# Local attention layers on one Trainium2 core: a list scheduler in place of a written order, the softmax maximum folded in by a matmul, one exponential per 128x512, the small norm steps on GpSimd

## The chip, the core and the metric

The kernel runs on one core of a Trainium2 chip. A core has five engines with queues of their own: TensorE (PE; PEld is its loading of weights), VectorE (DVE), ScalarE (ACT), GpSimd (POOL) and SyncE (SP), which here issues nearly all DMAs. Each engine takes its instructions in the order in which the program wrote them, and waits on semaphores for the others. The metric is the device time of one execution in microseconds (us); lower is better. Line numbers such as L804 are lines of the kernel before.

## What is computed

There are 32 batch elements of 128 rows and 128 features. First comes a cross attention with 16 heads of 8 features, with a layer norm in front, and then a stack of 6 layers. Each layer is a local attention with 16 heads of 64 features in windows of 32 rows, and a feed forward part. The core of the reference, cut:

```python
x = x + xattn(layernorm(x), ctx, ctx, ...)
y = layernorm(x)
for i in range(6):
    y = attn_layer(shift_tokens(y), Wqkv[i], ...) + y     # second half of the features from the row before
    y = ffn_layer(shift_tokens(y), ...) + y               # layer norm, a * gelu(gate), second product
out = x + y

# attn_layer: q, k, v = split(x @ Wqkv)
q = l2norm(q) * qs;  k = l2norm(k) * ksc                  # per head of 64
q = q * cos * scale + rotate_half(q) * sin * scale        # and k with 1 / scale
sim = einsum(q, k_window) * 8                             # own and previous window: 64 keys
attn = softmax(where(mask, -max, sim))
out = einsum(attn, v_window) @ Wo
```

## The kernel before, in words

**Tiles and stages.** All activations stay in one SBUF tile (`xt`). The batch is cut into 8 groups of 4 elements. The cross attention goes first, group by group; then the layers, each over the 8 groups. A **unit** is one batch element in one layer: 192 units, four to a group. While a layer runs, the weights of the next are loaded and prepared (`prep_ops`).

**A unit.** The group's input is transposed once: `ax` (L656) writes the first 64 features by PE transposes (L660) and the second 64 by a matmul with a shift matrix (L661), which also moves them down by one row. The result is split into a high and a low part, so that each large product is three 128x512 matmuls (`split3`, L634: L636, L637, L638). Four products give queries and keys (`qk`); each is squared on ACT (L686), summed per head on DVE (L689), multiplied with two tables on DVE (L694, two instructions) and added crosswise on POOL (L700). The sums of squares become a reciprocal square root (`rsqrt_a`, `rsqrt_b`, `rsqrt_c`): a maximum on DVE (L118), Ln and Exp on ACT (L126, L128), and one Newton step of three instructions on DVE (L133, L135, L137). POOL scales the four chunks (L723), PE transposes them (L729), and ACT and DVE copy them out (L735, L739, L744, L746).

**Values.** Value and output projection are one product (`yy`); ACT copies it out (L762) and 16 DMAs of 64 KB spread each window's rows over the partitions (L769).

**Softmax.** Half a unit is a block of 128x512 scores: a bf16 matmul writes the mask (L781), and 32 matmuls of 32 columns add the scores (L786). DVE takes the negated maximum of each 64 (L793). ACT runs eight exponentials of 128x64, each with its own bias column and its own accumulated sum (L804). DVE takes reciprocals (L809), POOL scales (L813), DVE transposes in 32x32 blocks (L817), and PE multiplies with the values in 28 matmuls (L830).

**Feed forward.** After four units the residual is added (L848), a DMA shifts the second half of the features by one row (L851, 127 partitions), the row norm follows (L857 to L880; its square root goes through the same helpers), then PE transposes, three gate products with Gelu on ACT (L910), three more products, and the second matrix (L935). After each Gelu group L912 loads the table set `natural_log_exp_and_others` again, which the kernel also loads at its start (L140).

**What sets the order.** The tables `OFF`, `GOFF`, `OFF1`, `GOFF1` (L38 to L84) give each operation of a unit a place on a time line, written out by hand. `push` puts functions with their times in a heap, and `drain` calls them in the order of time; each engine's queue follows from that. Buffers come from pools that rotate: five PSUM banks for products (`pj`), two for scores (`pscr`), one for the attention output (`pou`).

```python
        else:
            nc.scalar.activation(y, y, AF.Exp, scale=-0.5)
...
            for q in range(4 * half, 4 * half + 4):
                nc.scalar.activation(pr[:, q, :], scv[:, q, :], AF.Exp, bias=mx[:, q:q + 1],
                                     accum_out=ls[:, q:q + 1])
...
            if i == 2:
                nc.scalar.preload_act_table_set("natural_log_exp_and_others")
```

Of the kernel before, what the change touches and what calls it, by code (L numbers as in the profile page):

```python
# [8 lines left out]
F32 = mybir.dt.float32  # L9
# [7 lines left out]
P = 128  # L17
# [5 lines left out]
NRT = 8  # L23
NYT = 4
NKB = 3
NQT = 3
EWD = (1,)
STORE = 0.4
MP1 = [23.0 + 1.2 * i for i in range(8)]
WV1, DH1, DL1 = [20.85, 22.05], 0.15, 0.3  # L30
PREP0, PREPT = 10.0, 7.0
SHIFT = 6.0
FFT = 7.0
MP = [31.47, 31.72, 31.97, 32.22, 32.47, 32.72, 32.97, 33.22]
WV, BIAS, DH, DL = [24.4, 25.4], 16.4, 0.06, 0.14
T1 = 7.0
NI1 = 180
OFF1 = dict(  # L38
    sc=[[0, 2, 26, 28], [32, 34, 73, 75], [93, 95, 139, 141], [154, 159, 170, 172]],
    mx=[[1, 3, 27, 29], [33, 35, 74, 76], [94, 96, 140, 142], [158, 164, 171, 173]],  # L40
    sb=[[4, 5, 30, 31], [36, 37, 77, 78], [97, 98, 143, 144], [165, 168, 174, 175]],
    ex=[[39, 41, 44, 48], [99, 100, 101, 102], [151, 152, 155, 160], [187, 189, 192, 196]],
    tp=[[42, 46, 51, 55], [126, 127, 128, 129], [153, 157, 163, 167], [190, 194, 199, 203]],
    st=[[45, 50, 54, 57], [130, 132, 134, 135], [156, 162, 178, 179], [193, 198, 202, 205]],
    pa=[[49, 53, 82, 83], [131, 133, 136, 137], [161, 166, 186, 188], [197, 201, 218, 220]],
    oT=[[84], [138], [191], [223]], pb=[[145], [146], [195], [227]], rl=[[147], [148], [200], [232]],
    at=[[149], [150], [204], [236]],
)
GOFF1 = dict(
    ldc=[-101], gst=[-121, -120], gr0=[-119], gr1=[-117, -116], gr2=[-115, -114, -113], xa=[-118], xb=[-112],  # L50
    px=[-89], pxe=[-88], pcx=[-100], pce=[-99], pk=[-77], ke=[-76], kd=[-75], pq=[-74, -73, -71, -67],
    qe=[-72, -69, -65, -62], qd=[-70, -66, -63, -60], pv=[-55], vt=[-11], td=[-110], ab=[-109, -108], ln=[-4],
    mkb=[-56], tbm=[-3], p2=[238], aT=[249], pw=[265], rs=[266], hst=[267, 268], hr0=[269], hr1=[292, 296],
    hr2=[299, 301, 302], xf1=[270], xf2=[303],
)
T = 13.3
NI = 331
OFF = dict(
    qk=[[0, 1, 30, 31], [79, 80, 107, 108], [153, 154, 194, 195], [244, 245, 284, 285]],
    sq=[[2, 6, 32, 36], [81, 85, 109, 113], [155, 159, 196, 200], [246, 250, 286, 290]],  # L60
    ss=[[7, 11, 37, 41], [86, 90, 114, 118], [160, 164, 201, 205], [251, 255, 291, 295]],
    ta=[[3, 8, 33, 38], [82, 87, 110, 115], [156, 161, 197, 202], [247, 252, 287, 292]],
    tb=[[4, 9, 34, 39], [83, 88, 111, 116], [157, 162, 198, 203], [248, 253, 288, 293]],
    add=[[5, 10, 35, 40], [84, 89, 112, 117], [158, 163, 199, 204], [249, 254, 289, 294]],
    rs0=[[42], [119], [206], [296]], rs1=[[62, 63], [141, 142], [219, 220], [313, 314]],
    rs2=[[64, 65, 66], [143, 144, 145], [221, 222, 223], [315, 316, 317]],
    mul=[[67, 68, 69, 70], [146, 147, 148, 149], [224, 225, 226, 227], [318, 319, 320, 321]],
    tq=[[100, 102, 104, 136], [181, 183, 185, 228], [268, 270, 272, 275], [354, 356, 358, 381]],
    ev=[[101, 103, 105, 137], [182, 184, 186, 229], [269, 271, 273, 276], [355, 357, 359, 382]],
    ew=[[106, 138], [187, 230], [274, 277], [360, 383]],  # L70
    y=[[127, 128, 131, 150], [235, 236, 239, 281], [304, 305, 308, 328], [374, 375, 376, 407]],
    yt=[[129, 132, 134, 151], [237, 240, 242, 282], [306, 309, 311, 329], [384, 386, 388, 408]],
    dm=[[130, 133, 135, 152], [238, 241, 243, 283], [307, 310, 312, 330], [385, 387, 389, 409]],
    sc=[[124, 125, 178, 179], [216, 217, 260, 261], [301, 302, 347, 348], [390, 391, 426, 427]],
    mx=[[126, 180], [218, 262], [303, 349], [392, 428]],
    ex=[[165, 166, 212, 213], [256, 257, 297, 298], [343, 344, 377, 378], [422, 423, 451, 452]],
    rl=[[167, 214], [258, 299], [345, 379], [424, 453]], pl=[[168, 215], [259, 300], [346, 380], [425, 454]],
    PT=[[231, 232], [322, 323], [402, 403], [470, 471]], av=[[263, 264], [350, 351], [429, 430], [506, 507]],
)
GOFF = dict(  # L80
    ax=[-53], axh=[-52], axl=[-51], res=[508], psh=[564], fst=[565, 596], xn1p=[598], frs0=[597], frs1=[655, 656],
    frs2=[657, 658, 683], xn2p=[684], ptn=[735], xnh=[736], xnl=[737], gate=[831, 832, 833], gel=[834, 835, 836],
    pa=[850, 851, 853], um=[852, 854, 855], w2=[869, 870, 871, 872], res2=[873],
)  # L84

@with_exitstack
def body(ctx: ExitStack, tc: tile.TileContext, x, ctx_in, fside, mask, xWq, xWk, xWv, xWo, xtw,
# [5 lines left out]
    NG = B // GB  # L93
    HC = [(0, 128), (128, 128), (256, HID - 256)]
    RT = HC[2][1]

    const = ctx.enter_context(tc.tile_pool(name="const", bufs=1))
    small = ctx.enter_context(tc.tile_pool(name="small", bufs=4))

    nC = cst.shape[1] - 512  # L100
    cs = const.tile([P, nC], F32, tag="cs", name="cs")
# [5 lines left out]
    shift = cs[:, 516:644]  # L107
    identb = const.tile([P, P], BF16, tag="identb", name="identb")
    nc.vector.tensor_copy(identb, ident)
    maskb = const.tile([P, 512], BF16, tag="maskb", name="maskb")  # L110
    xt = const.tile([P, B, P], F32, tag="xt", name="xt")

    def rsqrt_a(src, n, eps, floor, tagp):
        v = small.tile([P, n], F32, tag=tagp + "v", name=tagp + "v")
        if eps is not None:
            nc.vector.tensor_scalar(v, src, eps, None, op0=ALU.add)
        else:
            nc.vector.tensor_scalar(v, src, floor, None, op0=ALU.max)  # L118
        y = small.tile([P, n], F32, tag=tagp + "y", name=tagp + "y")
        t = small.tile([P, n], F32, tag=tagp + "t", name=tagp + "t")  # L120
        return v, y, t

    def rsqrt_b(a, c):
        v, y, t = a
        if c == 0:
            nc.scalar.activation(y, v, AF.Ln)  # L126
        else:
            nc.scalar.activation(y, y, AF.Exp, scale=-0.5)  # L128

    def rsqrt_c(a, c):  # L130
        v, y, t = a
        if c == 0:
            nc.vector.tensor_tensor(t, y, y, op=ALU.mult)  # L133
        elif c == 1:
            nc.vector.scalar_tensor_tensor(t, v, -0.5, t, op0=ALU.mult, op1=ALU.mult)  # L135
        else:
            nc.vector.scalar_tensor_tensor(y, t, 1.5, y, op0=ALU.add, op1=ALU.mult)  # L137
        return y

    nc.scalar.preload_act_table_set("natural_log_exp_and_others")  # L140

    wch = ctx.enter_context(tc.tile_pool(name="wch", bufs=1))
    wst = ctx.enter_context(tc.tile_pool(name="wst", bufs=1))
    pj = ctx.enter_context(tc.tile_pool(name="pj", bufs=5, space=PSUM))
    pscr = ctx.enter_context(tc.tile_pool(name="pscr", bufs=2, space=PSUM))
    pou = ctx.enter_context(tc.tile_pool(name="pou", bufs=1, space=PSUM))

    heap = []
    seq = [0]

    def push(t, fn, a):
        heapq.heappush(heap, (t, seq[0], fn, a))
        seq[0] += 1

    def drain():
        while heap:
            _, _, fn, a = heapq.heappop(heap)
            fn(*a)

    NU = NG * GB  # L160
    ws = [None] * (L + 1)

    def prep_ops(l):
        w = ws[l] = {"qk": [None] * 4, "m": [None] * 4}
        wqk = Wqkv[l]
        V = {}

        def ld(i):
            if i == 0:
                V["w1r"] = wst.tile([P, 2 * HID], F32, tag="stg", name="w1r", bufs=2)  # L170
                nc.sync.dma_start(V["w1r"], W1[l])
            elif i == 1:
                V["col"] = wst.tile([P, 2], F32, tag="lgb", name="lgb")
                nc.sync.dma_start(V["col"][:, 0:1], ln_g[l].unsqueeze(1))
            elif i == 2:
                nc.sync.dma_start(V["col"][:, 1:2], ln_b[l].unsqueeze(1))
            elif i == 3:
                w["b1"] = wch.tile([P, 2, 3], F32, tag="b1c", name="b1c", bufs=2)
                nc.vector.memset(w["b1"], 0.0)
                for s in range(2):  # L180
                    nc.sync.dma_start(w["b1"][:, s, 0:2],
                                      b1[l, s * HID:s * HID + 2 * P].rearrange("(i p) -> p i", p=P))
            elif i == 4:
                nc.sync.dma_start(w["b1"][0:RT, :, 2], b1[l].rearrange("(s h) -> h s", s=2)[2 * P:HID])
            elif i == 5:
                w["w2"] = wch.tile([P, 3, P], F32, tag="w2", name="w2", bufs=2)
# [849 lines left out]
```

## Time and profile before

| | |
|---|---|
| median of 3 runs | 3326.27 us (3325.03 to 3327.11) |
| span of the profiled execution, first to last instruction | 3320.9 us |
| mean granted TensorE clock | 0.994 |
| ACT: exponentials (L804) and their accumulator reads | 3072 x 331 ns and 3072 x 225 ns |
| ACT: table loads at L910, L912 and L140 | 48 + 48 + 1, 1283 ns each |
| DVE: table products (L694) | 1536 x 681 ns |
| DVE: first step of the norm chain (L118) | 192 x 857 ns |
| PE: shift matmuls (L661) and their transposes (L660) | 384 x 298 ns and 192 x 293 ns |
| POOL: crosswise sum (L700), scaling (L723), softmax scaling (L813) | 768 x 1286, 768 x 1043, 384 x 1044 ns |
| DMA of the value rows (L769) | 3072 of 64 KB |

How to read it: the span is 5.4 us shorter than the median of the runs, which also counts what lies around the program. Durations are means over one profiled execution. The spans of PE overlap, since its matmuls are pipelined, and their ends are modelled: for PE the distance between starts tells more than the duration. An idle gap is put down to the semaphore that came last.

### The profile page before, as it was taken

How to read it: one execution, taken by the hardware profiler on the slowest of the kernel's cores; microseconds unless marked ns; L12 is line 12 of the kernel's file. 1: busy time of each engine (PE TensorE's matmuls, PEld its weight loads, DVE VectorE, ACT ScalarE, POOL GpSimd, SP SyncE). 2: the span in 40 equal slices, each digit the busy share in tenths (PEclk: the TensorE clock that was granted, in tenths of full speed). 3: DMA queues.
4: the chain of work that ended last, by engine and by line, in shares of the span. 5: the costliest groups of instructions: out<-in, count | busy, mean ns of one | idle time of the engine just before them, and what ended most of it. 6: DMA issues, size and time to landing. Idle time of an engine off the chain costs nothing.

```text
span 3320.9 us, 102077 instructions
## 1 busy us (share of the span) xinstructions
PE 3155.8 (95%) x35979; PEld 2389.3 (72%) x35979; DVE 2979.5 (90%) x6954; ACT 2834.9 (85%) x9983; POOL 2468.3 (74%) x2284
## 2 busy tenths in 40 slices
PE   8999899999999999999999999999999999999997
PEld 5555677777777777777777777777777777777775
DVE  6666899999999999999999998998999998999995
ACT  6776888898888898889898889898888898898895
POOL 5655777777787777787787787786787776777873
PEclk9999999999999999999999999999999999999998
DMA  2110333332333332233332333332333332333332
GB/s 61 33 37 12 77 87 82 79 74 71 75 83 86 78 74 72 72 85 84 77 77 71 75 83 81 79 77 68 79 83 76 84 76 64 77 82 81 82 83 62
DMA packets 217966, 243.80 MB, mean 73 GB/s; under 512 B 83534, under 2 KB 112498, under 8 KB 217458
## 3 DMA queue, kind: packets, MB, share of 16 engines
q1 hardware_dynamic: 217026, 236.93, 28.8%
q8 instruction: 288, 4.72, 0.6%
q14 instruction: 220, 1.80, 0.2%
q10 hardware_dynamic: 432, 0.34, 0.0%
HBM read 25.31 MB, written 4.19 MB: 9 GB/s over the span
## 4 chain that ended last, share of the span: by engine, by line
PE 49%; DVE 32%; ACT 8%; issue 4%; DMA 3%; SPq 2%; POOL 1%; ACTq 0%; DVEq 0%; POOLq 0%
DVE t L694 10%; PE pO L830 8%; PE ptq L729 7%; DVE ss L689 6%; PE sc L786 4%; DVE rnv L118 3%; PE pa L542 3%; PE pqk L636 3%; PE pqk L638 3%; ACT pr L804 3%; PE pqk L637 3%; DVE mx L793 2%; DVE PT L817 2%; SPq L769 2%; PE py L636 2%
## 5 line engine op out<-in xcount | busy, mean ns | idle before, releaser
L700 POOL TENSOR_TENSOR rt<-t,t 128x512 f32<-128x512 f32 x768 | 980.3, 1286 | 372.8 <-DVE t L694 330.8
L694 DVE TENSOR_TENSOR t<-pqk,tab 128x512 f32<-128x512 f32 x1536 | 983.3, 681 | 115.9 <-ACT sq L686 110.3
L804 ACT ACTIVATE pr<-sc,mx 128x64 f32<-128x64 f32 x3072 | 915.7, 331 | 61.2 <-DVE PT L817 53.0
L723 POOL TENSOR_TENSOR rt<-rt,rny 128x512 f32<-128x512 f32 x768 | 777.4, 1043 | 214.1 <-DVE rny L137 213.4
L804 ACT ACTIVATION_READ_ACCUMULATOR pr<-sc,mx 128x1 f32 x3072 | 691.9, 225 | 0.0
L689 DVE TENSOR_REDUCE ss<-sq 128x8 f32<-128x512 f32 x768 | 517.4, 674 | 0.0
L830 PE MATMUL pO<-ysh,PT 128*32 128x128 f32 x10752 | 416.9, 275 | 53.3 <-DVE PT L817 48.7
L813 POOL TENSOR_TENSOR pr<-pr,rl 128x512 f32<-128x512 f32 x384 | 400.8, 1044 | 89.2 <-DVE rl L809 89.2
L686 ACT ACTIVATE sq<-pqk 128x512 f32<-128x512 f32 x768 | 429.3, 600 | 24.6 <-PE pqk L638 12.5
L830 PEld LDWEIGHTS pO<-ysh,PT 128*32 128x32 f32 x10752 | 367.1, 110 | 97.6 <-DVE PT L817 72.1
L762 ACT COPY yt<-py 128x512 f32<-128x512 f32 x768 | 416.8, 614 | 21.2 <-PE py L638 17.2
L729 PE MATMUL ptq<-cs,rt 128*128 128x128 f32 x3072 | 409.8, 278 | 22.2 <-DVE t L694 17.0
L729 PEld LDWEIGHTS ptq<-cs,rt 128*128 128x128 f32 x3072 | 334.5, 141 | 96.7 <-issue 52.5
L786 PE MATMUL sc<-kb,qT 128*32 128x128 f32 (+1 forms) x12288 | 375.1, 262 | 15.2 <-DVE kb L744 14.8
L786 PEld LDWEIGHTS sc<-kb,qT 128*32 128x32 f32 x12288 | 270.7, 109 | 114.5 <-issue 70.7
L636 PE MATMUL py<-mw,xsh 128*128 128x512 f32 x768 | 333.1, 434 | 8.9 <-ACT yt L762 5.8
L636 PE MATMUL pqk<-wqh,xsh 128*128 128x512 f32 x768 | 314.0, 409 | 4.8 <-ACT yt L762 2.8
L638 PE MATMUL py<-mw,xsl 128*128 128x512 f32 x768 | 301.9, 393 | 0.0
L638 PE MATMUL pqk<-wqh,xsl 128*128 128x512 f32 x768 | 300.9, 392 | 0.0
L637 PE MATMUL pqk<-wql,xsh 128*128 128x512 f32 x768 | 300.8, 392 | 0.0
L637 PE MATMUL py<-mw,xsh 128*128 128x512 f32 x768 | 300.6, 391 | 0.0
L735 ACT COPY qT<-ptq 128x512 f32<-128x512 f32 x384 | 208.1, 590 | 79.0 <-PE ptq L729 78.1
(168 smaller groups left out, 5756.8 us busy)
## 6 DMA issues: line engine op xcount, KB each, us to landing
ysh<-yt SPq DMA_DIRECT2D x3072, 64.0 KB
raw<-in_L_ffn_Wqkv SPq DMA_DIRECT2D x36, 256.0 KB
xsu<-xt SPq DMA_DIRECT2D x48, 127.0 KB
wor<-in_L_ffn_Wo SPq DMA_DIRECT2D x6, 512.0 KB
xt<-in_x SPq DMA_DIRECT2D x8, 256.0 KB
cx<-in_ctx SPq DMA_DIRECT2D x8, 256.0 KB
mk<-in_mask_BxS_ff SPq DMA_DIRECT2D x8, 256.0 KB
x_scratch<-xt SPq DMA_DIRECT2D x8, 256.0 KB
```

What stands on the lines that cost most here:

```text
L636: nc.tensor.matmul(pt, lh, rh, start=True, stop=False)
L637: nc.tensor.matmul(pt, lh, rl, start=False, stop=False)
L638: nc.tensor.matmul(pt, ll, rh, start=False, stop=True)
L686: nc.scalar.activation(V["sq", c], V["pp", c], AF.Square)
L689: nc.vector.tensor_reduce(V["ss"][:, c * 8:(c + 1) * 8], V["sq", c].rearrange("p (h d) -> p h d", d=64), axis=AX.X, op=ALU.add)
L694: nc.vector.tensor_tensor(V["t", k, c].rearrange("p h s d -> p h (s d)"), V["pp", c].rearrange("p (h d) -> p h d", d=64), w["tab"][:, c // ...
L700: nc.gpsimd.tensor_tensor(V["rt", c], V["t", 0, c], V["t", 1, c][:, :, ::-1, :], op=ALU.add)
L723: nc.gpsimd.tensor_tensor(rv, rv, V["rn"][:, c * 8:(c + 1) * 8].unsqueeze(2).to_broadcast([P, 8, 64]), op=ALU.mult)
L729: nc.tensor.transpose(V["ptq", c][:, k, :], V["rt", c][:, 2 * k:2 * k + 2].rearrange("p h s d -> p (h s d)"), ident)
L786: nc.tensor.matmul(sc[32 * c:32 * c + 32, :, wd, lo:64], qT[:, c, 32 * wd:32 * wd + 32], kT[:, c, :, 32 * wd - 32 + lo:32 * wd + 32], star ...
L804: nc.scalar.activation(pr[:, q, :], scv[:, q, :], AF.Exp, bias=mx[:, q:q + 1], accum_out=ls[:, q:q + 1])
L830: nc.tensor.matmul(pO[32 * wd:32 * wd + 32, j, :], PT[:, half, wd, blk, :], ysh[u][:, (2 * par + half) * P:(2 * par + half + 1) * P], star ...
```

## The change

Nearly every line of `body` is rewritten; what is computed stays. What is different:

- `Sched` takes every operation with its engine, what it reads and writes, a priority (the unit's number, shifted by the table `LATER`) and a cost from the table `COST`. It plays the program through once and at each moment starts the most urgent operation that is ready and for which a buffer is free. That order is the program's order, and the buffers handed out are the program's buffers. It counts 1.3 us for a change between the Gelu table (`G`) and the table of the exponentials and logarithms (`E`).
- PSUM: six banks for products, one for scores, one for the attention output.
- Scores: the negated maximum is written as float32r, and a matmul of the identity with the maximum, broadcast over 64 columns, adds it to the scores (`fold`). One exponential of 128x512 follows. DVE then sums each 64 (`sm`), in place of the accumulated sums.
- Norm chain: `newton` runs the maximum (or the added epsilon) and the Newton step, now four instructions, on POOL; Ln and Exp stay on ACT.
- The two table products become one DVE instruction of 128x1024 (`tab`).
- The second half of the keys is always copied by ACT.
- The shifted half lives in columns 128 to 192 of `xt`. The group input is transposed by four PE transposes. The shift by one row is now always a pair of DMAs, of 112 and of 15 partitions, once before the feed forward and once for the next layer.
- The table set `natural_log_exp_and_others` is loaded by name once, at the start; the line after the Gelus is not there.

```diff
-            nc.vector.tensor_scalar(v, src, floor, None, op0=ALU.max)
-            nc.scalar.activation(y, v, AF.Ln)
-            nc.scalar.activation(y, y, AF.Exp, scale=-0.5)
-            nc.vector.tensor_tensor(t, y, y, op=ALU.mult)
-            nc.vector.scalar_tensor_tensor(t, v, -0.5, t, op0=ALU.mult, op1=ALU.mult)
-            nc.vector.scalar_tensor_tensor(y, t, 1.5, y, op0=ALU.add, op1=ALU.mult)
+                nc.gpsimd.tensor_scalar(sl(v), cols(), floor, None, op0=ALU.max)
+            nc.scalar.activation(sl(y), sl(v), AF.Ln)
+            nc.scalar.activation(sl(y), sl(y), AF.Exp, scale=-0.5)
+            nc.gpsimd.tensor_tensor(sl(t), sl(y), sl(y), op=ALU.mult)
+            nc.gpsimd.tensor_tensor(sl(t), sl(t), sl(v), op=ALU.mult)
+            nc.gpsimd.tensor_scalar(sl(t), sl(t), -0.5, 1.5, op0=ALU.mult, op1=ALU.add)
+            nc.gpsimd.tensor_tensor(sl(y), sl(y), sl(t), op=ALU.mult)
...
-                nc.tensor.transpose(G["ptx"][0:64, k, :], xb[:, 0:64], ident)
-                nc.tensor.matmul(G["ptx"][64:128, k, :], xb[:, 64:128], shift, start=True, stop=True)
+        S.op("ax", lambda: tr4(pt.t, [xsg(g)[:, k] for k in range(GB)]), pri, [X[g], XS[g]], [pt], also=[hi, lo])
...
-            nc.vector.tensor_tensor(V["t", k, c].rearrange("p h s d -> p h (s d)"),
-                                    V["pp", c].rearrange("p (h d) -> p h d", d=64),
-                                    w["tab"][:, c // 2, k, :].unsqueeze(1).to_broadcast([P, 8, 64]), op=ALU.mult)
+            S.op("tab", lambda: nc.vector.tensor_tensor(
+                t.t.rearrange("p (k h d) -> p k h d", k=2, d=64),
+                pp.t.rearrange("p (h d) -> p h d", d=64).unsqueeze(1).to_broadcast([P, 2, 8, 64]),
+                tab.t[:, c // 2].unsqueeze(2).to_broadcast([P, 2, 8, 64]), op=ALU.mult), pri, [pp, tab], [t])
...
-            for q in range(4 * half, 4 * half + 4):
-                nc.scalar.activation(pr[:, q, :], scv[:, q, :], AF.Exp, bias=mx[:, q:q + 1],
-                                     accum_out=ls[:, q:q + 1])
+                S.op("fold", lambda: nc.tensor.matmul(sc.t, identr, mx.t.unsqueeze(2).to_broadcast([P, 8, 64]), start=False,
+                                                      stop=True, skip_group_check=True), pri, [mx, sc], [sc])
+                S.op("ex", lambda: nc.scalar.activation(pr.t, sc.t, AF.Exp), pri, [sc], [pr], table="E")
+                S.op("sm", lambda: nc.vector.tensor_reduce(sm.t, r8(pr), axis=AX.X, op=ALU.add), pri, [pr], [sm])
...
-            nc.sync.dma_start(xsu[1:P], xg[0:P - 1, :, 64:128])
+            nc.sync.dma_start(xt[g][1:113, :, 128:192], xt[g][0:112, :, 0:64])
+            nc.sync.dma_start(xt[g][113:P, :, 128:192], xt[g][112:P - 1, :, 0:64])
...
-            if i == 2:
-                nc.scalar.preload_act_table_set("natural_log_exp_and_others")
```

The core of the scheduler's step, with the charge for a table:

```python
                occ = o.occ
                if o.table and o.table != table:
                    table = o.table
                    occ += 1.3
                    if table == "G":
                        hold = 3
...
                end = t + o.done + occ - o.occ
                free[e] = t + occ
                heapq.heappush(times, free[e])
                order.append((t, o))
```

## The prediction

> **What bounds the kernel now.** I read the busy shares first, then the steady stretch, then the order of matmuls inside it, because busy shares of four engines between 74% and 95% do not say which one sets the pace.
>
> ```profile
> PE 3155.8 (95%) x35979; PEld 2389.3 (72%) x35979; DVE 2979.5 (90%) x6954; ACT 2834.9 (85%) x9983; POOL 2468.3 (74%) x2284
> ```
>
> The profiled execution spans 3320.9 us; the median of the runs is 3326.27, so 5.4 us lie around the span. From 700 to 2700 us only the layer stage runs. In that window the groups give:
>
> ```profile
> 700.00:2700.00 2000.00, 1928.65 (x23101) 1494.78 (x23100) 1869.55 (x3775) 1769.69 (x6447) 1540.77 (x1416) 1.00 0.32 77
> ```
> ```profile
> L813 POOL TENSOR_TENSOR pr<-pr,rl 128x512 f32<-128x512 f32 x259 | 270.4, 1044 | 59.3 <-DVE rl L809 59.3
> L118 DVE TENSOR_SCALAR rnv<-ss 128x32 f32<-128x32 f32 x130 | 111.1, 855 | 4.5
> ```
>
> The columns of the first are the length, then busy time of PE, PEld, DVE, ACT, POOL. L813 runs twice per unit (one batch element in one layer), so 129.5 units pass in 2000 us: **15.44 us per unit**. Per unit DVE is busy 14.4 us, ACT 13.7, POOL 11.9. PE shows 14.9, but its spans overlap, so I take starts instead:
>
> ```profile
> 1498.28 0.40 PE L638 MATMUL pqk<-wqh,xsl 128*128 128x512 f32 x1
> 1498.52 0.39 PE L781 MATMUL sc<-maskb,identb 128*128 128x512 bf16 x1
> 1498.84 0.97 PE L786 MATMUL sc<-kb,qT 128*32 128x64 f32 x32
> 1499.74 0.50 PE L636 MATMUL py<-mw,xsh 128*128 128x512 f32 x1
> 1500.08 0.39 PE L637 MATMUL py<-mw,xsh 128*128 128x512 f32 x1
> 1500.31 0.40 PE L638 MATMUL py<-mw,xsl 128*128 128x512 f32 x1
> ```
>
> Full matmuls start 0.23 us apart. Behind the 32-column score matmuls the first pair is 0.34 apart instead (1499.74 to 1500.08). Over this window the gap from the last small matmul to the next full one is 0.20, against 0.03 within a small run; and a full matmul before unmasked small ones holds PE 0.32. So a change from small to full costs 0.17 + 0.11 = **0.28 us**, full to small 0.09. I priced the whole queue of the window with the median gap of each neighbour pair (clean means within small runs): 14.2 us per unit. PE has 14.2 us to issue and takes 15.44: it is the bound, with 1.24 us of waits on engines nearly as full (DVE 14.4, ACT 13.7).
>
> **The change, part by part** (per unit; 192 units, four to a group).
>
> *PE, work.* The shift matmuls of the group input go: before, four pairs of transpose and two-pass matmul take 4 x (0.23 + 0.16 + 0.20) = 2.37 us a group; four transposes at 0.11 take 0.44. That is -0.48 per unit. The fold of the maximum adds two 128x512 matmuls at 0.23: +0.46. Nothing in the trace shows one with a broadcast moving operand: below 0.23 there is no reason to go, the 0.43 spacing of the L435 matmuls would be the top (+0.4 more); it has the shape and type of L636, so 0.23.
>
> *PE, order.* The list scheduler interleaves more finely. In the instruction order, runs of one kind rise from 10.0 to 16.2 per unit; the two attention products stand apart (28 small matmuls each, before 56 together), and the halves of a score block are split. Small to full rises from 0.8 (0.5 after scores, 0.3 after the shift and weight pieces) to 3.85: 3.0 x 0.28 = +0.85. Full to small without a mask rises from 0.4 to 3.0: +0.23. Small to transpose (0.23 each) falls from 1.5 to 1.0, small to mask rises by 0.3, the rest nets to nothing: -0.05. Sum about +1.03; pricing the changed order instruction by instruction gives 15.25 against 14.2, **+1.05** with the two work terms. 1.3 us of the 15.25 rests on pairs not seen before, priced by their nearest.
>
> *ACT.* Eight exponentials with their accumulator reads take 0.29 each, 4.64 for 16; two 128x512 ones at the 0.49 of the squares take 0.98: -3.66. The key copy that leaves DVE adds 0.58. Then the table loads. The line that restored the combined table after each Gelu (L912) is gone, and the built order now has 231 loads before the Ln of the norm chains, 248 before exponentials and 48 before Gelu: 528 against 97, from 0.5 to about 2.8 per unit. What one costs:
>
> ```profile
> 1508.25 0.24 ACT L804 ACTIVATION_READ_ACCUMULATOR pr<-sc,mx 128x1 f32 x1
> 1508.51 1.28 ACT L910 ACT_TABLE_LOAD   x1
> 1509.81 1.83 ACT L910 ACTIVATE u<-pg,b1c 128x512 f32<-128x512 f32 x3
> 1511.65 1.28 ACT L912 ACT_TABLE_LOAD   x1
> 1512.95 1.07 ACT L735 COPY qT<-ptq 128x512 f32<-128x512 f32 x2
> ```
>
> From the end of one operation to the start of the next are 1.32 us (1508.49 to 1509.81), and neighbours that otherwise overlap by 0.11 no longer do: 1.43. So 2.25 x 1.43 = +3.2, and ACT stays at 13.7 - 3.66 + 0.58 + 3.2 = **13.8**: the relief is spent. The Trainium skill ("ScalarE: Activation LUTs", What ACT_TABLE_LOAD costs) puts a switch of sets at about 2.66 us, load and drain; that would add 6.0, make ACT 16.6 and the bound at 17.5 or more a unit. The row decides for 1.43. The same page (Table sets) has one set with both exp and ln, and the trace agrees: before, Ln and Exp follow each other 0.26 us apart with no load.
>
> *DVE and POOL.* DVE loses the norm chain (0.855 + 0.490 + 0.243 + 0.192 = 1.78, and some 0.56 for the group's), a key copy 0.69, and 0.25 from one double-width product per chunk; the sums of the exponentials add 1.25. About 12.4. POOL gets five steps of 128x32 and, per group, five of 128x4. No row has them: MEMSETs of 1 to 16 columns take 0.10 to 0.12; the line through 128x256 (0.616) and 128x512 (1.043) gives 0.24 and 0.20, which I take; as slow as DVE's they would be 1.8. +1.45, to 13.4. The skill speaks against it ("GPSIMD Engine Reference", Performance versus the Vector engine: elementwise about twice as slow there). Double the fastest DVE passes (0.235, 0.146, 0.191, 0.191) is 1.53, about the same sum. But the median rnv takes 0.85 against a fastest 0.235, so the DVE steps mostly stood and waited; "SBUF — State Buffer" (Who interferes with whom) names a port that DVE and GpSimd lock for each other, which fits.
>
> That chain now holds POOL's queue: the Ln and the Exp stand behind loads, so 1.4 to 2.9 us more pass between its first and second step, while the median order leaves POOL 2.2 us of other work there. Behind the waiting step stand the scalings of four rotated chunks, on which PE's transposes wait. Cover: PE has 20 us of its own work between a unit's projections and its first transpose. I charge this nothing alone; without that cover it is up to 1.5 a unit.
>
> *SP.* The shift of rows becomes two DMAs, of 112 and 15 rows, and is made for the next layer too: 192 issues for 48. At 0.6 to 0.76 us each +90 us on a queue whose 3072 value copies take 1,800 of 3320: hidden; behind a shift that waits for its residual stand value copies of the next unit, two units of buffers ahead. The copy of 127 rows takes 10.4 us from issue to use at the end (3288.37 to 3298.74); the value copies in the chain of waits take 2.6 to 2.9. I take 3, so the exposed tail falls 8 us; 0 if it stays. The cross attention keeps its work and has no added loads: 0, within 8 us either way. One score bank instead of two, and six projection banks instead of five, are inside the waits below.
>
> **The sum.** PE's issue is 15.25. For the waits I keep the measured 1.24: ACT is as full as before (13.8), POOL fuller (13.4), DVE emptier, and the loads are in no cost of the scheduler's table. 16.5 per unit, 192 x 1.05 = +202; 3320.9 + 5.4 + 202 - 8 = **3520 us**.
>
> **The rivals.**
> - *Loads hidden* (0.2). The order leaves a median 4.3 us of PE work between a projection or transpose and the reuse of its bank, and ACT needs about 0.9 of it. Then waits fall to some 0.4: 15.65, +40, and 3360 with the tail. Against it: the score bank has only 2.3 us between fold and reuse.
> - *Loads stop PE* (0.18). Ln and Exp with both loads hold ACT 3.2 us while every bank waits. If each pair, 1.2 per unit, adds 1 us on top of the old waits, 17.7: 3750.
> - *Faster* (0.12). One mechanism: at the 3.85 places where full matmuls follow small ones, the gap is a disguised wait and not a price. It decides when the 0.28 is under 0.08 and waits are at 0.4: then 14.5 + 0.5 = 15.0, 3235. Against it: the 0.20 and 0.34 are nearly constant over the window. At 15.4 it breaks even.
> - *Nothing moves* (0.03): small gaps and waits cancel, about 3326.
> - The forecast has 0.47, with waits from 0.8 to 1.9: 3435 to 3645.
>
> A measurement of this kernel can tell about 0.2% from no change. Faster 0.12, same 0.03, slower 0.85. The range cuts off the faster case and the upper end of the loads case: 3340 to 3740.
>
> **What would show it.** Right: about 528 table loads of 1.28 us, ACT busy near 80 to 90%, POOL idle before its second norm step on ACT, PE gaps of 0.20 and 0.34 behind small matmuls some 3.9 times a unit, a fold at 0.23 spacing, units of 16.5 us. Wrong: units under 15.4, PE's priced queue well under 15.25, no loads before Ln and Exp, or ACT under 70%.

## The result, and the profile after

| | before | changed |
|---|---|---|
| median | 3325.65 us (4 runs, 3324.52 to 3327.11) | 3717.3 us (4 runs, 3709.44 to 3729.36) |
| ratio | 1 | 1.1181, 95% interval 1.116 to 1.1203 |
| profiled execution, its span | 3320.9 us | 3729.36 us, span 3727.6 us |
| mean granted TensorE clock | 0.994 | 0.975 |

The change costs 392 us. The forecast was 3520, 194 us more than before: the sign was right, the size was half. Line numbers from here on are those of the changed kernel, except where the kernel before is named. First the busy shares of the changed kernel's page, then its answer for 700 to 2700 us (length; busy PE, PEld, DVE, ACT, POOL; granted clock):

```profile
PE 3395.6 (91%) x35979; PEld 2387.0 (64%) x35979; DVE 2613.5 (70%) x5157; ACT 2821.4 (76%) x4846; POOL 2736.2 (73%) x3528
```
```profile
700.00:2700.00 2000.00, 1834.27 (x20235) 1305.82 (x20234) 1431.14 (x2291) 1563.99 (x2642) 1510.00 (x1940) 0.98 0.30 71
```

Every engine is busy for a smaller share of the time than before: all of them wait for each other. POOL's softmax scaling (L817, twice a unit) runs 227 times in the window, so 113.5 units pass: 17.62 us a unit for 15.44. Per unit ACT is busy 1563.99 / 113.5 = 13.8, POOL 13.3, DVE 12.6. The table loads are there, in the costliest groups of the page:

```profile
L376 ACT ACT_TABLE_LOAD x231 | 296.4, 1283 | 4.1
L379 ACT ACT_TABLE_LOAD x225 | 288.7, 1283 | 4.0
...
L872 ACT ACT_TABLE_LOAD x48 | 61.6, 1283 | 0.9
L814 ACT ACT_TABLE_LOAD x23 | 29.5, 1283 | 6.1 <-PE bank__67 L812 3.9
```

L376 is the Ln of the norm chain, L379 its Exp, L872 Gelu, L814 the softmax exponential. How they reach PE is seen in selected rows of one passage of the timeline (start, duration, engine, line, instruction; in brackets the idle time before it and what ended it):

```profile
1429.76 1.28 ACT L376 ACT_TABLE_LOAD   x1
1429.80 0.29 POOL L373 TENSOR_SCALAR rv__18192<-ss__17849 128x32 f32<-128x32 f32 x1
...
1430.52 0.19 DVE L816 RECIPROCAL sm__18174<-sm__18174 128x8 f32<-128x8 f32 x1
...
1431.06 0.23 ACT L376 ACTIVATE ry__18194<-rv__18192 128x32 f32<-128x32 f32 x1
1431.31 1.28 ACT L379 ACT_TABLE_LOAD   x1
1432.60 0.23 ACT L379 ACTIVATE ry__18194<-ry__18194 128x32 f32<-128x32 f32 x1
...
1432.91 0.24 POOL L382 TENSOR_TENSOR rw__18207<-ry__18194 128x32 f32<-128x32 f32 x1 [2.83 <-ACT ry__18194 L379]
1433.11 1.26 POOL L748 TENSOR_TENSOR rt__18149<-t__18190 128x512 f32<-128x512 f32 x1
1434.33 1.04 POOL L817 TENSOR_TENSOR pr__18095<-pr__18095,sm__18174 128x512 f32<-128x512 f32 x1
1434.40 0.60 ACT L814 ACTIVATE pr__18178<-bank__67 128x512 f32<-128x512 f32 x1
1435.40 0.71 DVE L819 STREAM_TRANSPOSE PT__18243<-pr__18095 128x512 f32<-128x512 f32 x1 [1.82 <-POOL pr__18095 L817]
1436.17 0.30 PE L829 MATMUL bank__68<-ysh__17703,PT__18243 128*32 128x128 f32 x1 [3.07 <-DVE PT__18243 L819]
```

ACT spends 1429.76 to 1432.83 on two loads and two operations of 0.23 us. POOL has done the first norm step (L373) and stands 2.83 us before the second (L382). Behind it in POOL's queue is the softmax scaling L817 of another block. Its last operand was ready at 1430.71 (the reciprocal L816), and it starts at 1434.33; so the transpose L819 is late, and PE stands 3.07 us before the products with the values. And PE pays once more. The same answer by windows, for that stretch and the two after it:

```profile
1429.50:1436.20 6.70, 3.21 (x31) 2.03 (x22) 4.88 (x8) 6.38 (x11) 3.79 (x7) 1.00 0.03 7
1436.50:1439.90 3.40, 3.40 (x43) 2.08 (x36) 3.40 (x6) 0.00 (x0) 3.15 (x6) 0.50 0.00 0
1439.90:1450.00 10.10, 10.10 (x144) 7.07 (x143) 7.63 (x13) 8.36 (x16) 9.00 (x9) 1.00 0.29 67
```

After the stall the granted clock is 0.50 for 3.4 us (third column from the right). The trace has 39 stretches at 0.50, of 3.4 us or longer, for 7 before; (1 - 0.975) x 3727.6 = 93 us of clock are lost for 20.

**Where the 407 us between the two spans are.** The first mask matmul of the layers comes at 363.6 us for 332.6 (+31: the cross attention). From there to the last mask matmul pass 3327.4 us for 2941.4 (+386, 2.0 a unit). The rest to the end takes 36.6 for 46.9 (-10).

### The profile page after: what moved, and what is told of

Read it like the earlier page. It is cut to its first block, busy times and chain, and to the rows that moved or that the text cites. A ratio compares the mean times of both kernels' runs of the same rounds, so it can differ in the third digit from the quotient of the medians.

```text
span 3727.6 us, 95891 instructions
## 1 busy us (share of the span) xinstructions
PE 3395.6 (91%) x35979; PEld 2387.0 (64%) x35979; DVE 2613.5 (70%) x5157; ACT 2821.4 (76%) x4846; POOL 2736.2 (73%) x3528
## 3 DMA queue, kind: packets, MB, share of 16 engines
q14 instruction: 175, 1.43, 0.1%
## 4 chain that ended last, share of the span: by engine, by line
PE 43%; ACT 18%; DVE 15%; POOL 11%; issue 10%; DMA 3%; SPq 1%; ACTq 0%; POOLq 0%; DVEq 0%
PE bank__68 L829 5%; PE bank__67 L803 4%; ACT L376 3%; ACT L379 2%; PE bank__67 L687 2%; PE bank__67 L812 2%; PE bank__62 L403 1%; PE bank__63 L403 1%; PE bank__65 L409 1%; PE bank__61 L403 1%; SPq L784 1%; PE bank__61 L409 1%; PE bank__64 L403 1%; PE bank__67 L799 1%; PE bank__65 L403 1%
## 5 line engine op out<-in xcount | busy, mean ns | idle before, releaser
L799 PE MATMUL bank__67<-maskb,identb 128*128 128x512 bf16 x384 | 150.4, 392 | 36.7 <-ACT pr__25002 L814 3.1
L799 PEld LDWEIGHTS <-identb 128*128 128x128 bf16 x384 | 37.2, 97 | 77.4 <-issue 76.9
L839 DVE TENSOR_TENSOR xt<-bank__68,xt 128x512 f32<-128x512 f32 x48 | 32.6, 679 | 2.8 <-PE bank__68 L829 2.6
L770 ACT COPY kb__85<-bank__63 64x512 f32<-64x512 f32 x36 | 20.8, 578 | 11.0 <-PE bank__63 L409 11.0
L770 ACT COPY kb__85<-bank__65 64x512 f32<-64x512 f32 x31 | 17.8, 574 | 12.0 <-PE bank__65 L409 11.9
L770 ACT COPY kb__85<-bank__62 64x512 f32<-64x512 f32 x39 | 22.5, 577 | 3.5 <-PE bank__62 L409 3.4
L770 ACT COPY kb__85<-bank__64 64x512 f32<-64x512 f32 x32 | 18.4, 575 | 7.4 <-PE bank__64 L409 7.4
L770 ACT COPY kb__85<-bank__61 64x512 f32<-64x512 f32 x29 | 16.7, 578 | 8.7 <-PE bank__61 L409 8.6
L895 DVE TENSOR_TENSOR xt<-bank__61,xt 128x512 f32<-128x512 f32 x10 | 6.9, 692 | 23.2 <-PE bank__61 L891 23.2
L771 ACT COPY kb__85<-bank__62 64x512 f32<-64x512 f32 x39 | 22.7, 581 | 0.6
L895 DVE TENSOR_TENSOR xt<-bank__62,xt 128x512 f32<-128x512 f32 x9 | 6.2, 691 | 23.1 <-PE bank__62 L891 23.1
L895 DVE TENSOR_TENSOR xt<-bank__66,xt 128x512 f32<-128x512 f32 x11 | 7.6, 691 | 20.9 <-PE bank__66 L891 20.9
L771 ACT COPY kb__85<-bank__63 64x512 f32<-64x512 f32 x36 | 20.9, 581 | 0.6
L770 ACT COPY kb__84<-bank__63 64x512 f32<-64x512 f32 x34 | 19.8, 584 | 1.8 <-PE bank__63 L409 1.8
L771 ACT COPY kb__84<-bank__63 64x512 f32<-64x512 f32 x34 | 19.8, 581 | 0.6
L770 ACT COPY kb__84<-bank__62 64x512 f32<-64x512 f32 x33 | 19.2, 581 | 1.4 <-PE bank__62 L409 1.4
L770 ACT COPY kb__84<-bank__64 64x512 f32<-64x512 f32 x31 | 18.0, 580 | 2.3 <-PE bank__64 L409 2.3
L770 ACT COPY kb__84<-bank__61 64x512 f32<-64x512 f32 x33 | 19.2, 582 | 0.5 <-PE bank__61 L409 0.5
```

The lines of the kernel that those rows point to most:

```text
L770: S.op("evk", lambda: nc.scalar.copy(d.t[0:64, :, 0, :], p3()[0:64]), pri, [pt], [d])
L771: S.op("evk", lambda: nc.scalar.copy(d.t[64:128, :, 1, :], p3()[64:128]), pri, [pt], [d])
L799: nc.tensor.matmul(sc.t, identb, maskb, start=True, stop=True)
```

## The experiments

In the table, "unit" is 2000 us over the units in the window; "issue" is the sequence of PE's matmuls in the trace, priced as in the prediction with the gaps of the kernel before; "waits" is the difference, and holds what a lower clock costs too. ACT is its busy time per unit. From e5 on every run except e11 and e13 has e1's edit as well. e12 has e1's issue in the table: its matmuls are e1's, in the same order, and its trace lacks some of their records.

| run | us, median | ratio to before (95%) | table loads | unit | issue | waits | ACT |
|---|---|---|---|---|---|---|---|
| before | 3325 | 1 | 97 | 15.44 | 14.20 | 1.24 | 13.7 |
| changed | 3717 | 1.116 to 1.120 | 528 | 17.62 | 15.4 | 2.2 | 13.8 |
| e1_no_loads | 3398 | 1.021 to 1.024 | 97 | 15.75 | 15.33 | 0.42 | 10.8 |
| e2_before_loads | 3717 | 1.116 to 1.120 | 553 | 17.70 | 14.21 | 3.5 | 16.8 |
| e3_one_load | 3487 | 1.046 to 1.050 | 324 | 16.19 | 15.30 | 0.9 | 12.2 |
| e4_told | 3553 | 1.067 to 1.070 | 510 | 16.74 | 15.28 | 1.46 | 13.6 |
| e5_scores_whole | 3349 | 1.006 to 1.009 | 97 | 15.44 | 14.62 | 0.82 | 10.7 |
| e6_no_fold | 3497 | 1.050 to 1.053 | 97 | 16.33 | 14.77 | 1.56 | 14.2 |
| e7_norm_on_dve | 3552 | 1.067 to 1.070 | 97 | 16.53 | 15.32 | 1.2 | 10.8 |
| e8_like_with_like | 3345 | 1.004 to 1.007 | 97 | 15.56 | 14.52 | 1.04 | 10.8 |
| e9_wide_runs | 3121 | 0.938 to 0.940 | 97 | 14.55 | 14.15 | 0.40 | 10.7 |
| e10_xattn_bank | 3375 | 1.014 to 1.017 | 97 | 15.50 | 14.65 | 0.85 | 10.7 |
| e11_wide_runs_loads | 3564 | 1.071 to 1.074 | 525 | 16.95 | 14.05 | 2.9 | 13.6 |
| e12_act_spread | 3687 | 1.107 to 1.110 | 97 | 17.24 | 15.33 | 1.9 | 14.1 |
| e13_told_late | 3672 | 1.102 to 1.105 | 531 | 17.17 | 15.14 | 2.0 | 13.7 |
| e14_norm_late | 3551 | 1.063 to 1.069 | 97 | 16.53 | 15.34 | 1.2 | 10.8 |

### What the loads cost

**e1_no_loads**, the changed kernel with the line of the kernel before put back:

```diff
-            S.op("gel", lambda: nc.scalar.activation(u.t[0:n], pg.t[0:n], AF.Gelu, bias=b1c.t[0:n, 1, i:i + 1]), pri,
+            S.op("gel", lambda: (nc.scalar.activation(u.t[0:n], pg.t[0:n], AF.Gelu, bias=b1c.t[0:n, 1, i:i + 1]), i == 2 and nc.scalar.preload_act_table_set("natural_log_exp_and_others")), pri,
```

> The changed kernel with the combined table set loaded by name after each third Gelu: 97 table loads for 528, and the same order of everything else on every engine. Loads theory (each Ln and Exp pair with its two loads holds ACT 3.2 us, PE runs out of banks and stands): the 17.7 us unit loses at least the 1.2 us that are over the forecast, and some of the old waits too, since ACT falls from 13.8 to about 10.6 us a unit: 15.7 to 16.4 us, 3365 to 3500 us in all. Order theory (the finer interleaving of matmuls and the single score bank make the waits, the loads lie beside other work): the unit stays over 17.2, the time over 3630 us.

3398 us: 319 of the 392 us were the loads. The same operations as in the passage above, in e1's timeline:

```profile
1335.14 0.23 ACT L376 ACTIVATE ry__18209<-rv__18207 128x32 f32<-128x32 f32 x1 [0.37 <-POOL rv__18207 L373]
1335.40 0.23 ACT L379 ACTIVATE ry__18209<-ry__18209 128x32 f32<-128x32 f32 x1
...
1335.72 0.24 POOL L382 TENSOR_TENSOR rw__18222<-ry__18209 128x32 f32<-128x32 f32 x1 [0.60 <-ACT ry__18209 L379]
...
1339.28 0.30 PE L829 MATMUL bank__68<-ysh__17717,PT__18258 128*32 128x128 f32 x1 [1.16 <-DVE PT__18258 L819]
```

POOL stands 0.60 us for 2.83, PE 1.16 for 3.07. And the window:

```profile
700.00:2700.00 2000.00, 1976.65 (x22651) 1425.87 (x22650) 1594.68 (x2558) 1367.30 (x2640) 1681.10 (x2158) 1.00 0.33 78
```

The clock is back at 1.00, and of 15.75 us a unit 15.33 are PE's own queue. The theory that the finer order makes the waits fell; what the order costs is the longer queue itself.

**e2_before_loads**, the kernel before without its L912:

```diff
-            if i == 2:
-                nc.scalar.preload_act_table_set("natural_log_exp_and_others")
```

> The kernel before without the line after the Gelus: 553 loads for 97 in the written order, nothing else moved. Loads theory: ACT rises from 13.7 by 2.4 x 1.43 to 17.1 us a unit and becomes the bound, with some wait on top: 17.2 to 17.8 us, 3660 to 3780 us, so the loss of that line alone would cost as much as the whole change. Order theory (loads mostly lie in idle time of ACT): under 16.2 us, below 3475 us.

3717 us: losing that one line costs the old kernel as much as the whole change costs. ACT is its bound, 16.8 of 17.7 us. There the second norm step is on DVE, and DVE's wait for ACT before it (L133 for L128) rises from 3 to 216 us of the 2000. That the two sums agree to the microsecond is chance.

**e3_one_load**, in which the Exp of the norm needs no load:

```diff
+            nc.scalar.preload_act_table_set("natural_log_exp_and_others")
             nc.scalar.activation(sl(y), sl(v), AF.Ln)
```

> The changed kernel with the combined set loaded by name ahead of each Ln: the load ahead of the Exp of the norm goes, 324 loads for 528, order the same. Loads theory: the gain is about in proportion, 204 of the 431 loads that can go: a little under half of what the kernel with 97 loads gains, 3540 to 3610 us. If it is the double hold of 3.2 us that stops PE and a single one of 1.7 us is covered by the banks, nearly all of the gain comes back: 3400 to 3480 us. Order theory: over 3650 us.

3487, just above the second case: 204 loads fewer give back 230 us, the next 227 only 89. Whether the first ones are dearer because there are more of them, or because they stand right behind another load, this run does not tell.

**e4_told**, again with the changed kernel's loads, lets the scheduler charge 1.3 us for each change between Ln, exponentials and Gelu, instead of between Gelu and the rest.

```diff
-                    table = o.table
-                    occ += 1.3
+                    gel = gel or o.table == "G"; table = o.table
+                    occ += 1.3 if gel else 0.0
...
-        S.op(names[1], f1, pri, [v], [y], table="E")
+        S.op(names[1], f1, pri, [v], [y], table="L")
```

> The changed kernel with the scheduler told of the loads: Ln, the exponentials and Gelu count as three table sets, 1.3 us at each change once the first Gelu has run. 510 loads stay. Loads theory in the form that the stall comes from holds that the plan does not know: the order puts other work in PE's queue there and gets back a part, 3550 to 3670 us. In the form that ACT's time itself is the price: no change, 3680 to 3740 us. Order theory: no change either.

3553: 164 us come back although 510 loads stay, and waits fall from 2.2 to 1.46. A plan that knows of the loads stands about as well with them as the old order stood with its full ACT.

**e11_wide_runs_loads**: the best order found (e9, below), with e1's edit taken back.

> As the kernel with wide runs, without the named load after the third Gelu: 525 loads for 97 in the same order. Loads theory: the loss is ACT's time and the holds, in whatever order: 150 to 330 us more than with 97 loads, 3300 to 3530 us. If it was only the interleaved order that left PE open to the holds: under 100 us more.

3564 for 3121: 442 us more, and over the range of 150 to 330. No order tried here hides loads that were not planned. The way by which they reach PE depends on the order: here PE waits for the maximum (L828 for L827, 96 us of the 2000 for 6 in e9) and for the score bank (L815 for the exponential L830, 88 us for none), and 133 us of clock are lost for 17 in e9.

### By which route

**e12_act_spread** is e1 with four squares and two query copies issued twice, in the same order.

```diff
-            S.op("sq", lambda: nc.scalar.activation(sq.t, pp.t, AF.Square), pri, [pp], [sq])
+            S.op("sq", lambda: [nc.scalar.activation(sq.t, pp.t, AF.Square) for _ in range(2)], pri, [pp], [sq])
...
-                    S.op("evq", lambda: nc.scalar.copy(d.t, pt.t), pri, [pt], [d])
+                    S.op("evq", lambda: [nc.scalar.copy(d.t, pt.t) for _ in range(2)], pri, [pt], [d])
```

> As the changed kernel with 97 table loads, in the same order, but six of ACT's 128x512 operations of a unit are issued twice (the four squares, the two query copies; the second writes the same values again). ACT gets 6 x 0.49 = 2.9 us a unit more, spread out, nearly what the 2.25 added table loads take (3.2). If the fill of ACT makes PE's waits, whatever fills it: 290 us more than 3398, 3640 to 3720 us. If it is the long holds, in which ACT serves nobody for 1.3 to 3.2 us: ACT still has room at 13.7 of 15.8, 3400 to 3480 us.

3687: 289 us more with hardly a long hold. My theory that it takes long holds to cost so much fell. But this run has a route of its own: DVE waits for squares (L739 and L743 for L738) rise from 95 to 203 us of the 2000 (122 in the changed kernel), while POOL's wait at L382 is 68. So it shows that a full ACT can cost this much, not that the loads cost it in this way.

**e14_norm_late** is e1 in which the Exp of the 128x32 norm reaches POOL through a DMA within SBUF; ACT gets no work.

```diff
-            nc.scalar.activation(sl(y), sl(y), AF.Exp, scale=-0.5)
+            nc.scalar.activation(sl(y), sl(y), AF.Exp, scale=-0.5); n == 32 and nc.sync.dma_start(y2(), sl(y))
...
-            nc.gpsimd.tensor_tensor(sl(t), sl(y), sl(y), op=ALU.mult)
+            nc.gpsimd.tensor_tensor(sl(t), y2(), y2(), op=ALU.mult)
```

> The changed kernel with 97 loads and the same order, but the result of the norm's Exp reaches POOL's second step by way of a 16 KB DMA within SBUF, which costs some 2 us of landing and nothing on ACT. POOL theory: the wait before that step rises from 0.2 to about 2.2 us a unit, as with all loads, and brings most of the loss by itself: 3580 to 3720 us. Fill theory: ACT is as empty as before, so under 80 us more than 3398, below 3480 us.

3551, 152 us more than e1: between the theories. POOL's wait at that step is 180 us of the 2000 for the DMA (225 for ACT in the changed kernel, 27 in e1). At the same place in the order as in the passages above (lines are two higher here):

```profile
1383.47 0.24 POOL L384 TENSOR_TENSOR rw__18287<-ry__18273 128x32 f32<-128x32 f32 x1 [2.34 <-DMA ry__18273<-ry__18273]
...
1384.90 1.04 POOL L819 TENSOR_TENSOR pr__18174<-pr__18174,sm__18253 128x512 f32<-128x512 f32 x1
...
1386.74 0.42 PE L831 MATMUL bank__68<-ysh__17779,PT__18323 128*32 128x128 f32 x1 [2.61 <-DVE PT__18323 L821]
```

PE's waits for the transposed block are 48 us of the 2000, for 10 in e1 and 68 in the changed kernel. So lateness of one 128x32 result, which stops POOL's queue, costs 152 us with an empty ACT. Value copies held up by the added DMAs explain little of it: PE's waits for them are 5 us of the 2000 for none in e1, ACT's 25 for 28.

**e13_told_late** tells the scheduler that Ln and Exp give their results 1.43 us later, not that they hold ACT.

```diff
-    mxs=("POOL", .18, .18), ln=("ACT", .27, .24), ep=("ACT", .27, .24), nw=("POOL", .20, .20),
+    mxs=("POOL", .18, .18), ln=("ACT", .27, 1.67), ep=("ACT", .27, 1.67), nw=("POOL", .20, .20),
...
-    eps=("POOL", .18, .18), lnf=("ACT", .22, .21), epf=("ACT", .22, .21), nwf=("POOL", .20, .20), xn2=("POOL", 1.08, 1.05),
+    eps=("POOL", .18, .18), lnf=("ACT", .22, 1.64), epf=("ACT", .22, 1.64), nwf=("POOL", .20, .20), xn2=("POOL", 1.08, 1.05),
```

> The changed kernel, in which the scheduler's table says that the results of the norm's Ln and Exp come 1.43 us later each; that they also hold ACT is not told. 531 loads stay. POOL theory (in the trace POOL waits 227 us of 2000 before its second norm step for the Exp behind its loads, and the softmax scaling that stands behind it in POOL's queue comes late for the products with the values): that wait falls under 0.7 us a unit from 2.0, and 100 to 200 us come back, 3510 to 3620 us. Fill theory (ACT's time, wherever it is spent, makes PE's waits): less than 60 us come back, over 3655 us.

3672: the wait at L382 falls to 82 us as expected, but only 45 us come back. POOL waits elsewhere instead, and PE's waits for the score bank rise from 23 to 54 us (L799, for L814). So there are two routes, the late norm and the full ACT. Each can make a large part of the loss alone (152 us, and 289 with late squares among them), they overlap, and their shares in the 319 us stay open.

### The other parts of the change

**e6_no_fold** and **e7_norm_on_dve** undo one part each in e1. In e6 `COST` has 2.31 us for the exponentials. In e7 all five steps of `newton` change in this manner, and their engine in `COST` too.

```diff
-                S.op("fold", lambda: nc.tensor.matmul(sc.t, identr, mx.t.unsqueeze(2).to_broadcast([P, 8, 64]), start=False,
-                                                      stop=True, skip_group_check=True), pri, [mx, sc], [sc])
-                S.op("ex", lambda: nc.scalar.activation(pr.t, sc.t, AF.Exp), pri, [sc], [pr], table="E")
-                S.op("sm", lambda: nc.vector.tensor_reduce(sm.t, r8(pr), axis=AX.X, op=ALU.add), pri, [pr], [sm])
+                def ex():
+                    for c in range(8):
+                        nc.scalar.activation(r8(pr)[:, c, :], r8(sc)[:, c, :], AF.Exp, bias=mx.t[:, c:c + 1], accum_out=sm.t[:, c:c + 1])
+                S.op("ex", ex, pri, [sc, mx], [pr, sm], table="E")
```
```diff
-            nc.gpsimd.tensor_tensor(sl(t), sl(y), sl(y), op=ALU.mult)
+            nc.vector.tensor_tensor(sl(t), sl(y), sl(y), op=ALU.mult)
```

> As the changed kernel with 97 table loads, but without the fold: eight exponentials of 128x64 a block with their own bias and accumulated sum, as in the kernel before; the sum on DVE goes. ACT rises from 10.8 by 3.66 to 14.4 us a unit, PE's priced queue falls by 0.6 to 14.7, DVE falls to 11.3. If ACT's relief is what took the waits away: waits are back at 1.0 to 1.4, 15.7 to 16.1 us, 3390 to 3470 us. If the fold's place on PE costs more than the relief gives: waits stay near 0.4, 15.1 us, about 3275 us.

> As the changed kernel with 97 table loads, but the small norm steps run on DVE instead of GpSimd, the same five instructions. POOL falls from 13.3 to 11.8 us a unit, DVE rises from 12.6 to between 13.5 and 14.4. PE is the bound at 15.3 either way: within 25 us of 3398. If the norm step that waits for ACT holds POOL's queue and so PE's transposes: up to 0.4 a unit less, 3320 to 3375 us. If it holds DVE's: 3425 us or more.

The fold is worth 99 us: without it PE's queue is 0.56 us shorter, but the waits are 1.56, above the range. The norm steps on POOL are worth 154 us, which I had not expected: on DVE they make it 14.5 us a unit for 12.6, since steps that can take 0.15 to 0.17 us (the fastest tenth) take 0.31 to 0.47 in the mean; PE's waits for DVE's transposes and maxima rise from 17 to 58 us of 2000. What makes them long is POOL:

```profile
1322.09 1.27 POOL L748 TENSOR_TENSOR rt__17308<-t__17366 128x512 f32<-128x512 f32 x1
...
1322.46 0.95 DVE L382 TENSOR_TENSOR rw__17391<-ry__17371 128x32 f32<-128x32 f32 x1
...
1323.96 0.14 DVE L385 TENSOR_TENSOR rw__17391<-rw__17391,rv__17360 128x32 f32<-128x32 f32 x1
```

The first DVE step begins beside a running POOL instruction and ends 0.05 us after it; the second has POOL idle. Of the 960 steps of 128x32 in e7, 362 took over 0.30 us. All of them began beside a running POOL instruction, and all but two ended 0.03 to 0.06 us after it; those that began with POOL idle took 0.17 us in the mean. On POOL the same steps are steady: in e1, L373 takes 0.283 to 0.289 us in eight of ten cases.

**e5_scores_whole** makes, in e1, the two halves of a score block one operation; **e8_like_with_like** adds to it a preference for matmuls of the same width (second diff).

```diff
-                S.op("sc0", lambda: scores(0), pri, [q, k], [sc], also=[pr])
-                S.op("sc1", lambda: scores(1), pri, [q, k, sc], [sc])
+                S.op("sc0", lambda: (scores(0), scores(1)), pri, [q, k], [sc], also=[pr])
```
```diff
+                        if best is None:
+                            best = (o, got)
+                        if e != "PE" or (o.name in SMALL) == small:
+                            best = (o, got)
+                            break
```

> As the changed kernel with 97 table loads, but the two halves of a score block are one operation of the scheduler (its cost 1.06 us), so the mask and 32 score matmuls stay together. In the order small to full changes fall from 3.8 to 2.5 a unit, full to small from 2.95 to 1.25; priced with the gaps of the kernel before, PE's queue falls from 15.27 to 14.64 us. Price theory (a change of matmul kind is a real cost in PE's queue): 0.63 x 192 = 121 us less than the 3398 us with 97 loads, 3277, within 3245 to 3310, below both kernels. Disguised wait theory (the gaps are waits that go elsewhere): 3380 to 3410 us. One score bank held longer could add up to 40 us.

> As the kernel with whole score blocks and 97 loads, and the scheduler takes, among ready PE operations within 3 units of priority, one of the same width (32 columns or full) as the last: small to full changes 1.5 a unit, priced queue 14.51. Price theory: 25 us less than with whole score blocks alone, about 3250 us; if the postponed operations bring waits of 0.2 to 0.5 a unit, 3290 to 3350 us.

PE's queue fell as priced, to 14.62 and 14.52, but only 49 and 53 us came of the 121 and 146: waits rose from 0.42 to 0.82 and 1.04, in e8 for the maximum (L825 for L824 there, 31 us) and for the transposed block (24 us).

**e9_wide_runs** keeps both (the preference within half a unit), tells the scheduler the price of a change of width, has e10's edit, and moves priorities, a few costs and one kept-back bank (`KEEP`) until long runs of small matmuls end in transposes:

```diff
+                if e == "PE":
+                    if small:
+                        occ += .2 if o.name in TRANS or o.name == "sc0" else 0.0 if o.name in SMALL else .28
...
-LATER = dict(ax=-0.5, mul=-1.5, pl=-0.5, evk=0.5, sc0=3, axl=-0.25, mx=-1, xsb=3)
+LATER = dict(ax=0, mul=-1, pl=-0.5, evk=1.5, sc0=2.5, axl=-0.25, mx=-1, xsb=3, y=2, av=4, qk=-1, xtr=2, tq=1, ex=-0.5, xn1=2)
```

> Built on the kernel with whole score blocks and 97 loads. The scheduler also counts 0.28 us where a full matmul follows small ones and 0.2 where a transpose does, prefers an operation of the same width within half a unit of priority, and takes the products with the values up to 4 units later (other priorities moved by half a unit to two). In the order small to full changes fall from 2.5 to 0.15 a unit, full to small from 1.25 to 0.05, small to transpose rises from 0.8 to 1.9; the priced queue falls from 14.64 to 14.10 us. Price theory: with waits of 0.4 to 0.8 a unit is 14.5 to 14.9, 3130 to 3230 us, below the kernel before. If the late products only trade changes for waits on buffers, as whole score blocks did in part (72 of 121 us given back): 3290 to 3350 us.

```profile
700.00:2700.00 2000.00, 1990.42 (x24580) 1585.60 (x24580) 1712.86 (x2768) 1472.15 (x2868) 1815.79 (x2337) 1.00 0.36 84
```

3121 us, 6.1% below the kernel before (0.938 to 0.940) and a little under the range: queue 14.15, waits 0.40. The edits were made together, so what each gave is not shown. The fullest engine after PE is POOL, with 1815.79 of 2000.

**e10_xattn_bank** is e5 with the transposed sums of the cross attention in a projection bank:

```diff
-        oT, pb, rl = Buf("pr"), Buf("sc"), Buf("xrl")
+        oT, pb, rl = Buf("pr"), Buf("pj"), Buf("xrl")
```

> Only one line against the kernel with whole score blocks: in the cross attention the transposed sums go to a projection bank instead of the one score bank, the layers stay as they are. The first mask matmul of the layers came at 366 us there and at 333 in the kernel before. If the single score bank, in which one batch element's cross attention waits for the last, makes this: it comes at 335 to 345 and the time falls by 20 to 30 us to about 3322. If it is the order of the cross attention or the earlier weight work: within 8 us of 3349.

Refuted: the first mask matmul comes at 392.4 us, 26 later still. In e9, which has this edit and other priorities, it comes at 334.0. So this bank is not what holds the cross attention up; which of e9's other edits brings it back was not tried.

## Why the prediction was right and wrong

- **PE's queue, work and order (+1.05): right.** The changed kernel's sequence prices at 15.4, and e1 takes 15.75 with 0.42 of waits, so the price is real. Small to full changes number 3.8 a unit; the gap to the full matmul is 0.20 us and the next one 0.34, in every run. The fold is somewhat dearer than the 0.23: behind a full matmul it holds PE 0.215 us, but nearly three of four stand behind transposes or small matmuls, and there it holds PE 0.30 to 0.32. (The parts listed under order and work add up to 1.01, not 1.03; the 1.05 did not come from them.) The rival "faster", that these gaps are disguised waits, falls with e1 and e9; e5 and e8 alone gave back well under half of their price.
- **ACT stays at 13.8, POOL 13.4, DVE 12.4: right** (13.8, 13.3, 12.6). 528 loads of 1.283 us; the POOL steps of 128x32 take 0.22 to 0.29 us for the 0.24 estimated, and the reading that the DVE steps before mostly stood and waited is right (e7 shows for what). The Trainium skill ("ScalarE: Activation LUTs", What ACT_TABLE_LOAD costs) has some 2.66 us for a switch of sets, a load of about 1.283 and a drain of about 1.38, which would have put ACT at 16.6. Only the load shows here: from the end of one operation to the start of the next are 1.31 us in the median.
- **The waits, kept at 1.24: this step failed.** It said "ACT is as full as before". The two busy times are alike, but the old order was written around that ACT; the new one was planned for an ACT of 10.8, and 3.0 us of loads came on top unplanned. The waits are 2.2. Of the 213 us by which the rise of the span, 407, is above the forecast's 194, the layers have 184 (386 for 202), most of it these waits. Where the plan knows of the same fill they come near the old value: 1.46 in e4, 1.56 in e6. Where it doesn't, they are 1.9 to 2.9 (changed, e12, e13, e11).
- **The chain that holds POOL's queue, charged "nothing alone": wrong.** I looked only at the scalings that PE's transposes need, which have 20 us of cover. What is late is the softmax scaling L817 behind the waiting step, with no such cover: PE's waits for the transposed block are 68 us of the 2000 for 10 in e1. e14 prices this lateness at 152 us, 0.8 a unit.
- **The clock: missed.** The sum has no term for it. Unplanned stalls lowered it: 74 us more lost clock, contained in the waits.
- **The cross attention, "0, within 8 us": wrong**, +31. The tail, -8: right, -10; the shift's DMAs land in 2.5 and 2.1 us.
- Of the rivals, "loads stop PE" gave 17.7 a unit and 3750 and came nearest in size, but partly by luck: it has every bank wait for ACT, and PE's waits for the score bank are only 23 us of the 2000. Its way is seen in e11. "Loads hidden" (15.65 a unit, waits of 0.4) is nearly what e1 shows, once there are no loads to hide.

## What to carry to other kernels

A wait measured under one order is not a property of the kernel: when an order is planned with a cost table, look for costs that the table lacks and price them as unhidden. A long-latency step that is moved to another engine's in-order queue must be charged with what stands behind it there, not only with its own consumers. Keep one table set for Ln and Exp by loading it by name after every switch: here that one line is worth 319 us in one order, 392 in another and 442 in a third.

## What the runs showed of the hardware

- A short PE stall is enough to lose the clock. In the layers of the changed kernel every stretch of a granted clock of 0.50 lasts 3.4 us, or two to three times that, and follows a stall of 1.6 to 3.9 us from one matmul's start to the next. The Trainium skill ("TensorE: Matmul & The Clock Gate", Part 1) gives the half rate "after ≥1 idle window (~3.4µs)"; here less was often enough: of 14 gaps in which PE was idle 2.0 to 2.5 us, nine were followed by such a stretch, and of 34 of 1.5 to 2.0 us, nine.
- Small steps of 128x32 have a mean of 0.22 to 0.29 us on POOL and 0.31 to 0.47 on DVE (e7), although DVE's fastest tenth takes 0.15 to 0.17: on DVE they can stand until a running POOL instruction ends. The kernel before shows it too: 310 of its 576 steps at L118, L133 and L135 took over 0.30 us, and all 310 began beside a running POOL instruction.
- A second, identical ACT instruction that writes the same tile starts 0.63 us after the first, where neighbours on different tiles start 0.49 apart (e12).
